# Edge sums of a graph layer: rows as three bfloat16 parts, one-hot matrices as the stationary side

## The chip, the core and the metric

The kernel runs on one core of a Trainium2 chip. The metric is the device time of one execution in microseconds (us). The core's engines are PE (TensorE, matrix products), DVE (VectorE), ACT (ScalarE), POOL (GpSimd) and SP (SyncE, which here only issues DMAs). Each engine works through its own queue in order; semaphores tie the queues together. PE reads SBUF and writes PSUM, which has eight banks of 512 f32 per partition.

## What is computed

A layer of a graph network on 12500 nodes with 128 features and 200000 edges, sorted by destination. `h` is the layer norm of `x` with negative values cut off. Each node takes the mean of `h` over the sources of its incoming edges; four dense layers follow, and `x` is added.

```python
h = jnp.maximum(_layernorm(x, axis=-1), 0.0)
msgs = h[src]                                        # 200000 x 128
agg = segment_sum(msgs, dst, num_segments=n)
deg = segment_sum(ones, dst, num_segments=n)
agg = agg / jnp.maximum(deg, 1.0)[:, None]
y = relu(agg @ Wg + h @ Ws + bg)                     # 128
y = tanh(y @ W1 + b1)                                # 512
y = tanh(y @ W2 + b2)                                # 512
out = x + y @ W3 + b3                                # 128
```

## The kernel before

All is in `windowed`. (A second function, `general`, runs behind it if a flag says that the edges were not spread as assumed; with these inputs it is skipped.) The 200000 edges are cut into 1563 chunks of 128. Since edges are sorted and eight nodes take 128 edges on average, the edges of chunk c end at nodes near 8c; a window of 144 nodes around it (160 for raw chunks, 88 down to 40 for the last 67 chunks) holds them all.

Setup. x is read in pieces of up to 14 tiles of 128 nodes (line 217). `centre`, `factors` and `scale` (lines 161 to 176) make h out of it with whole-piece DVE operations and a Square and a Sqrt on ACT, and h goes as f32 rows of 512 B to a table in DRAM, `htab` (line 228). `indices` turns the lists of sources and destinations so that a chunk's indices stand in one column (`scol`, `dloc`), with PE transposes of a cast copy (lines 180 to 195).

Gathers. POOL fetches the 128 rows of one chunk with one indirect DMA (`gather`, line 290). No gather from the table may start before the table is written, so POOL is first given 80 chunks whose rows come from x itself ("raw" rows, line 132): ten groups of 8 chunks, every 40 chunks from chunk 256 on. Their layer norm is taken later, in the main loop, by the same `centre`, with the square on DVE (line 168). Behind the raw ones POOL gathers the other 1483 chunks in order, up to 40 chunks ahead of their use.

Aggregation. For a group of 8 chunks DVE builds one-hot matrices in f32 (`onehot`, line 327: edge by window position) and, chunk by chunk, adds the same comparison into a count per block of nodes (line 343). `lane`, the row of positions that is compared, lies in PSUM. PE (`add`) takes the gathered rows as the stationary side and the one-hot as the moving side, so sums come out as features by nodes, in PSUM, in the block's bank or, for chunks that lie across a border, in an edge bank. An f32 product is two instructions in the profile. `count` multiplies the counts by ones, so that every partition has the degrees, and takes the reciprocal; `merged` puts the bank and the edges together and multiplies by it.

Layers. Blocks are 23 of 512 nodes, then 256, 128, 128, 112 and 100. `part0` to `part4` are the dense layers; the pieces of their work are generators that the main loop advances between chunks. From chunk 1312 (QUICK) on a model of time, with `there` for the landing of a gather, decides what goes before the next chunk. The node's own h comes from htab (`own`, `hb`), is turned by PE (`own_turned`); x comes once more for the final addition (`own_part`). PE, ACT's own helpers and SP's DMAs are kept in program order; the other orders are the scheduler's. The flag comes from the sum of all degrees (`total`).

Of the kernel before, what the change touches and what calls it, by code (L numbers as in the profile page):

```python
# [31 lines left out]
P = 128  # L32
# [3 lines left out]
PIECE = 14  # L36
GRP = 8
NRAW = 10
# [4 lines left out]
LEAD = 16  # L43
QUICK = 1312

WINDOWS = ((0, 144), (1496, 88), (1536, 56), (1552, 40))
W_RAW = 160
W_MAX = max(W_RAW, *(w for _, w in WINDOWS))

# [6 lines left out]
def windowed(ctx, tc, x, src, dst, Wg, Ws, bg, W1, b1, W2, b2, W3, b3, out, flag):  # L56
# [12 lines left out]
    LAST = E - (NCH - 1) * P  # L69
    NCOL = NROW * CPR  # L70
    RAW1 = RAW0 + NRAW * STEP
    per = N * P // E
    assert D == P and H % P == 0 and per * E == N * P and RAW0 % GRP == STEP % GRP == 0
    assert all(c % GRP == 0 for c, _ in WINDOWS) and RAW1 <= WINDOWS[1][0]


    def raw(c):
        return RAW0 <= c < RAW1 and (c - RAW0) % STEP < GRP

    def first(w, span=per):
        return (span - w) // 2

    def window(c):
        if raw(c):
            return per * (c - c % GRP) + first(W_RAW, per * GRP), W_RAW
        w = [w for c0, w in WINDOWS if c0 <= c][-1]
        return per * c + first(w), w  # L90
# [12 lines left out]
    rows_in = ctx.enter_context(tc.tile_pool(name="rows_in", bufs=AHEAD))  # L103
    ps_c = ctx.enter_context(tc.tile_pool(name="ps_c", bufs=1, space=PSUM))
    ps_a = ctx.enter_context(tc.tile_pool(name="ps_a", bufs=2, space=PSUM))
    ps_m = ctx.enter_context(tc.tile_pool(name="ps_m", bufs=3, space=PSUM))
    ps_b = ctx.enter_context(tc.tile_pool(name="ps_b", bufs=1, space=PSUM))
# [11 lines left out]
    jp = const.tile([P, P], I32, name="jp")  # L119
    nc.gpsimd.iota(jp, pattern=[[1, P]], base=0, channel_multiplier=-1)  # L120
    lane_i = const.tile([P, W_MAX], I32, name="lane_i")
    nc.gpsimd.iota(lane_i, pattern=[[1, W_MAX]], base=0, channel_multiplier=0)
    row_i = const.tile([P, NROW], I32, name="row_i")
    nc.gpsimd.iota(row_i, pattern=[[per * CPR, NROW]], base=0, channel_multiplier=0)
    q_i = const.tile([P, CPR], I32, name="q_i")
    nc.gpsimd.iota(q_i, pattern=[[per, CPR]], base=first(WINDOWS[0][1]), channel_multiplier=0)

    raw_rows = []
    for g in range(NRAW):
        t = raws.tile([P, GRP, D], F32, name=f"raw{g}")  # L130
        for j in range(GRP):
            nc.gpsimd.indirect_dma_start(  # L132
                out=t[:, j, :], out_offset=None, in_=x,
                in_offset=bass.IndirectOffsetOnAxis(ap=rsrc[:, g, j : j + 1], axis=0),
            )
        raw_rows.append(t)

    ident = const.tile([P, P], F32, name="ident")
    nc.vector.tensor_scalar(ident, jp, 0.0, None, op0=ALU.is_equal)
    ones = const.tile([P, P], BF16, name="ones")  # L140
    nc.vector.memset(ones, 1.0)
    eps = const.tile([P, 1], F32, name="eps")
    nc.vector.memset(eps, EPS)

    shared = ps_c.tile([P, BLK], F32, name="shared")
    lane, row_f = shared[:, :W_MAX], shared[:, W_MAX : W_MAX + NROW]
    stats_raw = shared[:, BLK - 2 * NRAW * GRP :].rearrange("p (s c) -> p s c", s=2)
    assert W_MAX + NROW + 2 * NRAW * GRP <= BLK
# [5 lines left out]
    dloc = const.tile([P, NCOL], F32, name="dloc")  # L154

    def spread(f, k):
        return f[:, :, None].to_broadcast([P, k, D])

    def centre(pool, xt, k, stats, bufs=2):
        nc.vector.tensor_reduce(stats[:, 0], xt, AX.X, ALU.add)  # L162
        nc.vector.scalar_tensor_tensor(xt, spread(stats[:, 0], k), -1.0 / D, xt, op0=ALU.mult, op1=ALU.add)  # L163
        sq = pool.tile([P, k, D], F32, name=f"sq{k}", bufs=bufs)
        if bufs > 1:
            nc.scalar.activation(sq, xt, AF.Square)
        else:
            nc.vector.tensor_tensor(sq, xt, xt, op=ALU.mult)
        nc.vector.tensor_reduce(stats[:, 1], sq, AX.X, ALU.add)  # L169

    def factors(stats):
        nc.scalar.activation(stats[:, 1], stats[:, 1], AF.Sqrt, bias=eps, scale=1.0 / D)
        nc.vector.reciprocal(stats[:, 1], stats[:, 1])

    def scale(h, xt, k, stats):
        nc.vector.scalar_tensor_tensor(h, xt, 0.0, spread(stats[:, 1], k), op0=ALU.max, op1=ALU.mult)  # L176

    with tc.tile_pool(name="setup", bufs=1) as sp, tc.tile_pool(name="ln", bufs=2) as ln:

        def indices(name, a, pad, keep):  # L180
# [10 lines left out]
            for q0 in range(0, CPR, 4):  # L191
                p = ps_m.tile([P, 4, P], F32, name="pm")
                for q in range(4):
                    nc.tensor.transpose(p[:, q, :NROW], rf[:, (q0 + q) * P : (q0 + q + 1) * P], ident[:NROW, :NROW])  # L194
                keep(q0, p[:, :, :NROW].rearrange("p q r -> p r q"))


        def by_row(t):
            return t.rearrange("p (r q) -> p r q", q=CPR)

        def keep_src(q0, p):
            nc.vector.tensor_copy(by_row(scol)[:, :, q0 : q0 + 4], p)

        def keep_dst(q0, p):
            nc.vector.tensor_tensor(
                by_row(dloc)[:, :, q0 : q0 + 4], p, by_row(low)[:, :, q0 : q0 + 4], op=ALU.subtract
            )


        pieces = [(0, 4), (4, PIECE - 4)] + [(t, min(PIECE, NT - t)) for t in range(PIECE, NT, PIECE)]  # L210
        for i, (t0, k) in enumerate(pieces):
# [8 lines left out]
            if i == 1:  # L220
                indices("src", src, 0, keep_src)
            stats = ps_a.tile([P, BLK], F32, name="agg")[:, : 2 * k].rearrange("p (s t) -> p s t", s=2)
            xt = xt[:, :k]
# [4 lines left out]
            nc.sync.dma_start(htab[t0 * P : (t0 + k) * P, :].rearrange("(t p) d -> p t d", p=P), h[:, :k])  # L228

        low = sp.tile([P, NCOL], F32, name="low")
        nc.vector.tensor_copy(row_f, row_i)
        nc.vector.tensor_tensor(
            by_row(low), row_f[:, :, None].to_broadcast([P, NROW, CPR]), q_i[:, None, :].to_broadcast([P, NROW, CPR]),
            op=ALU.add,
        )
        for c0, w in WINDOWS[1:]:
            v = low[:, c0:]
            nc.vector.tensor_scalar(v, v, float(first(w) - window(c0 - 1)[0] + per * (c0 - 1)), None, op0=ALU.add)  # L240
        indices("dst", dst, 2 * N, keep_dst)
        steps, at = (t[:, RAW0:RAW1].rearrange("p (u k) -> p u k", k=STEP) for t in (dloc, low))
        nc.vector.scalar_tensor_tensor(
            steps[:, :, :GRP], rdst, float(first(WINDOWS[0][1]) - first(W_RAW, per * GRP)),
            at[:, :, :1].to_broadcast([P, NRAW, GRP]), op0=ALU.add, op1=ALU.subtract,
        )
# [43 lines left out]
    def gather(c):  # L290
        r = rows_in.tile([P, D], F32, name="rows")
        nc.gpsimd.indirect_dma_start(  # L292
            out=r, out_offset=None, in_=htab,
            in_offset=bass.IndirectOffsetOnAxis(ap=scol[:, c : c + 1], axis=0),
        )
        rows_t[c] = r
# [11 lines left out]
    def raw_stats(i):  # L308
        return stats_raw[:, :, i * GRP : (i + 1) * GRP]

    def raw_scaled(i):
        h = raw_rows[i]
        scale(h, h, GRP, raw_stats(i))
        for j in range(GRP):
            rows_t[RAW0 + i * STEP + j] = h[:, j]


    OHS = 4
    oh_bufs = [const.tile([P, GRP, WINDOWS[0][1]], F32, name=f"oh{i}") for i in range(OHS)]
    counts = {}  # L320

    def onehot(g):
        k = min(GRP, NCH - g * GRP)
        lo, w = window(g * GRP)
        is_raw = raw(g * GRP)
        oh = ed.tile([P, GRP, W_RAW], F32, name="ohr", bufs=2) if is_raw else oh_bufs[g % OHS]
# [5 lines left out]
        for c in range(g * GRP, g * GRP + k):  # L332
            lo, w = window(c)
            for b, (n0, m) in enumerate(blocks):
                a0, a1 = max(lo, n0), min(lo + w, n0 + m)
                if a0 < a1:
                    if b not in counts:
                        counts[b] = ed.tile([P, BLK], BF16, name="deg", bufs=3) if m > P else ed.tile(
                            [P, P], BF16, name="deg_s", bufs=4
                        )  # L340
                        nc.vector.memset(counts[b][:, :m], 0.0)
                    d = counts[b][:, a0 - n0 : a1 - n0]
                    nc.vector.scalar_tensor_tensor(  # L343
                        d, lane[:, a0 - lo : a1 - lo], dloc[:, c : c + 1], d, op0=ALU.is_equal, op1=ALU.add
                    )

    reach = [[] for _ in blocks]
    for c in range(NCH):
        lo, w = window(c)
        for b, (n, m) in enumerate(blocks):  # L350
            if lo < n + m and lo + w > n:
                reach[b].append(c)

# [674 lines left out]
```

## Time and profile before

| | |
|---|---|
| median of 3 runs | 1982.97 us (1982.76 to 1983.64) |
| profiled execution | 1985.8 us |
| its span, first to last instruction | 1983.9 us |
| PE, weight loads, DVE, ACT, POOL busy | 69%, 40%, 55%, 11%, 75% |
| mean granted PE clock | 0.893 |
| bytes read and written in HBM | 125.05 MB, 12.82 MB |
| queue of the gathers | 50016 packets, 102.53 MB, 20.5% of the 16 DMA engines' span |

A group in the profile has its line, engine, operation, output and inputs with their shapes and types, and the number of instructions; behind the bar stand the busy time in us and the mean ns of one, and behind the next the engine's idle time just before them, with what ended most of it. In the timeline a line starts with the start and the duration in us; in brackets stands the idle time before it and its releaser. PEld is the loading of a stationary side, POOL's record of an indirect DMA is its issuing and not the transfer.

### The profile page before, as it was taken

How to read it: one execution, taken by the hardware profiler on the slowest of the kernel's cores; microseconds unless marked ns; L12 is line 12 of the kernel's file. 1: busy time of each engine (PE TensorE's matmuls, PEld its weight loads, DVE VectorE, ACT ScalarE, POOL GpSimd, SP SyncE). 2: the span in 40 equal slices, each digit the busy share in tenths (PEclk: the TensorE clock that was granted, in tenths of full speed). 3: DMA queues.
4: the chain of work that ended last, by engine and by line, in shares of the span. 5: the costliest groups of instructions: out<-in, count | busy, mean ns of one | idle time of the engine just before them, and what ended most of it. 6: DMA issues, size and time to landing. Idle time of an engine off the chain costs nothing.

```text
span 1983.9 us, 16321 instructions
## 1 busy us (share of the span) xinstructions
PE 1374.1 (69%) x4838; PEld 793.6 (40%) x4838; DVE 1100.5 (55%) x2649; ACT 219.0 (11%) x352; POOL 1486.8 (75%) x1571
## 2 busy tenths in 40 slices
PE   0056547777778877777676776767767778888797
PEld 0034333434444444344333343333333434444466
DVE  7974856547766586536365363552644625554441
ACT  1100010011111111101001011010110111011022
POOL 7777777777777777777777777777777777777774
PEclk9999858799989898988989989989889898788697
DMA  8822222222222222222222222222222222222221
GB/s 214 234 52 63 55 52 63 53 69 52 69 69 68 54 69 69 69 53 68 69 53 68 53 69 68 53 69 60 62 68 53 69 76 64 60 74 64 53 61 42
DMA packets 120040, 139.10 MB, mean 70 GB/s; under 512 B 30743, under 2 KB 94099, under 8 KB 119749
## 3 DMA queue, kind: packets, MB, share of 16 engines
q0 software_dynamic: 50016, 102.53, 20.5%
q1 hardware_dynamic: 66766, 32.13, 5.9%
q10 hardware_dynamic: 3160, 3.31, 0.6%
q8 instruction: 40, 0.66, 0.1%
q14 instruction: 58, 0.47, 0.1%
HBM read 125.05 MB, written 12.82 MB: 69 GB/s over the span
## 4 chain that ended last, share of the span: by engine, by line
DMA 31%; issue 30%; PE 24%; POOL 8%; DVE 7%; ACT 1%; SPq 0%; POOLq 0%; DVEq 0%
DMA rows<-htab,scol 29%; PE pm L279 13%; POOL rows L292 8%; PE agg L279 7%; PE edge L279 3%; DVE deg L343 2%; PE pt L282 1%; DVE oh L327 1%; DMA xt<-in_x_dram 1%; DVE agg L162 1%; DVE h L176 1%; DVE agg L169 1%; DVE xt L163 0%; ACT h L303 0%; DVE rd L364 0%
## 5 line engine op out<-in xcount | busy, mean ns | idle before, releaser
L292 POOL DMA_INDIRECT rows<-htab,scol x1483 | 1408.6, 950 | 451.9 <-issue 280.1
L279 PE MATMUL agg<-oh,rows 128*128 128x144 f32 (+3 forms) x2122 | 562.7, 367 | 359.1 <-DMA rows<-htab,scol 327.0
L279 PEld LDWEIGHTS agg<-oh,rows 128*128 128x128 f32 x2122 | 392.2, 226 | 736.6 <-DMA rows<-htab,scol 549.2
L279 PE MATMUL pm<-h,w 128*128 128x512 f32 (+4 forms) x1344 | 653.7, 585 | 15.6 <-ACT h L303 15.6
L343 DVE SCALAR_TENSOR_TENSOR deg<-shared,dloc,deg 128x144 bf16<-128x144 f32 (+17 forms) x1921 | 565.7, 326 | 27.1
L327 DVE TENSOR_TENSOR oh<-shared,dloc 128x1152 f32<-128x1152 f32 (+2 forms) x186 | 245.2, 1318 | 207.4 <-PE agg L279 195.7
L279 PE MATMUL edge<-oh,rows 128*128 128x144 f32 (+2 forms) x844 | 223.7, 355 | 138.4 <-DMA rows<-htab,scol 136.8
L279 PEld LDWEIGHTS edge<-oh,rows 128*128 128x128 f32 x844 | 146.4, 212 | 303.0 <-DMA rows<-htab,scol 233.1
L279 PEld LDWEIGHTS pm<-h,w 128*128 128x128 f32 x1344 | 226.5, 208 | 33.7 <-ACT h L303 17.5
L544 DVE TENSOR_TENSOR o<-pt,xb 128x512 f32<-128x512 f32 x23 | 15.9, 691 | 284.8 <-PE pt L282 284.8
L303 ACT ACTIVATE h<-pm,b2c 128x512 f32<-128x512 f32 (+4 forms) x112 | 70.9, 633 | 704.1 <-PE pm L279 704.1
L362 DVE TENSOR_SCALAR rd<-pm 128x512 f32<-128x512 f32 (+4 forms) x28 | 17.4, 623 | 168.2 <-PE pm L279 168.2
L303 ACT ACTIVATE h<-pm,b1c 128x512 f32<-128x512 f32 (+4 forms) x112 | 70.4, 633 | 242.6 <-PE pm L279 242.1
L132 POOL DMA_INDIRECT raw<-in_x_dram,rsrc x80 | 77.3, 966 | 25.7 <-issue 23.8
L426 DVE TENSOR_TENSOR mT<-agg,sums 128x136 f32<-128x136 f32 (+6 forms) x57 | 15.4, 269 | 138.5 <-PE agg L279 134.7
L364 DVE RECIPROCAL rd<-rd 128x512 f32<-128x512 f32 (+4 forms) x28 | 81.8, 2920 | 0.0
L194 PE MATMUL pm<-ident,idx_f 98*128 98x98 f32 x32 | 6.0, 374 | 80.1 <-DVE idx_f L190 79.7
L306 ACT COPY hT<-pt 128x512 f32<-128x512 f32 (+1 forms) x25 | 14.4, 578 | 306.0 <-PE pt L282 293.6
L194 PEld LDWEIGHTS pm<-ident,idx_f 98*128 98x128 f32 x32 | 5.1, 224 | 80.7 <-issue 49.4
L303 ACT ACTIVATE h<-pm,bgc 128x512 f32<-128x512 f32 (+4 forms) x28 | 17.7, 633 | 166.0 <-PE pm L279 166.0
L279 PE MATMUL pm<-hT,ws 128*128 128x512 f32 (+4 forms) x56 | 29.7, 617 | 0.0
L279 PE MATMUL pm<-mT,wg 128*128 128x512 f32 (+4 forms) x56 | 29.1, 605 | 0.3 <-DVE mT L428 0.3
(66 smaller groups left out, 420.3 us busy)
## 6 DMA issues: line engine op xcount, KB each, us to landing
rows<-htab,scol POOLq DMA_INDIRECT x1483, 2.5
hb<-htab SPq DMA_DIRECT2D x24, 256.0 KB, 4.4
xb<-in_x_dram SPq DMA_DIRECT2D x23, 256.0 KB, 5.0
out_dram<-o SPq DMA_DIRECT2D x23, 256.0 KB, 2.7
htab<-h SPq DMA_DIRECT2D x6, 896.0 KB, 5.5
xt<-in_x_dram SPq DMA_DIRECT2D x5, 896.0 KB, 9.3
raw<-in_x_dram,rsrc POOLq DMA_INDIRECT x80, 5.2
w<-in_L_gnn_W_dram ACTq DMA_DIRECT2D x1, 1024.0 KB
```

The lines of the kernel that those rows point to most:

```text
L132: nc.gpsimd.indirect_dma_start(out=t[:, j, :], out_offset=None, in_=x, in_offset=bass.IndirectOffsetOnAxis(ap=rsrc[:, g, j : j + 1], axis=0),)
L162: nc.vector.tensor_reduce(stats[:, 0], xt, AX.X, ALU.add)
L169: nc.vector.tensor_reduce(stats[:, 1], sq, AX.X, ALU.add)
L176: nc.vector.scalar_tensor_tensor(h, xt, 0.0, spread(stats[:, 1], k), op0=ALU.max, op1=ALU.mult)
L279: tc.keep_in_program_order(nc.tensor.matmul(*a, **k))
L282: tc.keep_in_program_order(nc.tensor.transpose(*a, **k))
L292: nc.gpsimd.indirect_dma_start(out=r, out_offset=None, in_=htab, in_offset=bass.IndirectOffsetOnAxis(ap=scol[:, c : c + 1], axis=0),)
L303: tc.keep_in_program_order(nc.scalar.activation(*a, **k))
L327: nc.vector.tensor_tensor(oh[:, :k, :w], lane[:, None, :w].to_broadcast([P, k, w]), dloc[:, g * GRP : g * GRP + k][:, :, None].to_broadcas ...
L343: nc.vector.scalar_tensor_tensor(d, lane[:, a0 - lo : a1 - lo], dloc[:, c : c + 1], d, op0=ALU.is_equal, op1=ALU.add)
L362: nc.vector.tensor_scalar(rd[:, :m], dg[:, :m], 1.0, None, op0=ALU.max)
L364: nc.vector.reciprocal(rd[:, :m], rd[:, :m])
```

## The change

- The table holds each h as three bfloat16 parts whose sum is h, so a row is 3 x 128 bfloat16, 768 B. Layer norm statistics come from `bn_stats` and `bn_aggr`, tile by tile; ACT's ReLU with a scale and a shift per node makes h in PSUM, four tiles to a bank; ACT copies give the parts, DVE subtractions the rest. Pieces are 16 tiles.
- Raw groups are 11 in place of 10 (88 chunks); their norm goes by the same `moments` and a ReLU on ACT.
- Chunks come in groups of 13 (8 for raw ones; the last three groups have 6, 4 and 3). DVE builds one-hots in bfloat16 of 120 nodes from the group's first node (a per-group number, `firsts`, from a product with a matrix whose first row is ones). PE takes the one-hot as the stationary side and the gathered rows, with a column of ones behind them, as the moving side: sums come out as nodes by features, with the in-degree in the last column.
- When a group is complete DVE clips the degree at 256 (`in_deg`) and adds the three parts (`sums`); `put`, three chunks later (one, in the last 16), multiplies both by a 0/1 matrix (`place`, and its bfloat16 copy by ACT, `place_b`) that moves them to their nodes, features by nodes again, with the degree on every partition. DVE adds that to the block's `placed`, in SBUF. `merged` takes the maximum with 1, the reciprocal (into PSUM) and the product.
- A block is started when all groups that reach it have been put. The count per chunk, the edge banks and `count` are gone.
- The node's own h is made from x by ACT (`own_turned`); x is read once for that and for the final addition. Gathered rows lie in 6 fixed buffers of 8.

The core of the diff:

```diff
-PIECE = 14
+PIECE = 16
-NRAW = 10
+NRAW = 11
-LEAD = 16
+LEAD = 6
+KMAX = 13
+MARGINS = ((0, 68), (1496, 40), (1536, 24), (1552, 16))
+LAST = (6, 4, 3)
...
-    htab = dram.tile([NP, D], F32, name="htab")
+    htab = dram.tile([NP, SPLIT], BF16, name="htab")
...
+    def moments(pool, xt, k, mv):
+        st = pool.tile([P, PIECE, 6], F32, name="st")
+        for t in range(k):
+            nc.vector.bn_stats(st[:, t, :], xt[:, t, :D])
+            nc.vector.bn_aggr(mv[:, t, :], st[:, t, :])
+
+    def factors(mv, scale, off):
+        nc.scalar.activation(scale, mv[:, :, 1], AF.Sqrt, bias=eps)
+        nc.vector.reciprocal(scale, scale)
+        nc.vector.scalar_tensor_tensor(off, mv[:, :, 0], -1.0, scale, op0=ALU.mult, op1=ALU.mult)
...
-            centre(ln, xt, k, stats)
-            factors(stats)
-            h = ln.tile([P, PIECE, D], F32, name="h")
-            scale(h[:, :k], xt, k, stats)
+            moments(ln, xt, k, mv)
+            factors(mv[:, :k], rstd[:, t0 : t0 + k], shift[:, t0 : t0 + k])
+            h3 = ln.tile([P, PIECE, 3, D], BF16, name="h3")
+            for a in range(0, k, QUAD):
+                n = min(QUAD, k - a)
+                h = bank()
+                for t in range(n):
+                    at = t0 + a + t
+                    nc.scalar.activation(
+                        h[:, t, :], xt[:, a + t, :], AF.Relu, bias=shift[:, at : at + 1], scale=rstd[:, at : at + 1]
+                    )
+                for j in range(2):
+                    nc.scalar.copy(h3[:, a : a + n, j, :], h[:, :n, :])
+                    left = h3[:, a : a + n, 2, :] if j else h[:, :n, :]
+                    nc.vector.tensor_tensor(left, h[:, :n, :], h3[:, a : a + n, j, :], op=ALU.subtract)
...
     def onehot(g):
...
+        nc.vector.tensor_scalar(near[:, :k], dsts, first, None, op0=ALU.subtract)
...
         nc.vector.tensor_tensor(
             oh[:, :k, :w], lane[:, None, :w].to_broadcast([P, k, w]),
-            dloc[:, g * GRP : g * GRP + k][:, :, None].to_broadcast([P, k, w]), op=ALU.is_equal,
+            near[:, :k][:, :, None].to_broadcast([P, k, w]), op=ALU.is_equal,
         )
...
+        nc.vector.tensor_scalar(
+            place[:w, : hi - lo], shift_lane[:w, : hi - lo], float(lo), first[:w], op0=ALU.add, op1=ALU.is_equal
+        )
+        place_b = ed.tile([P, PLACE], BF16, name="place_b", bufs=4)
+        act.copy(place_b[:w, : hi - lo], place[:w, : hi - lo])
...
+    def add(c):
...
+        pe.matmul(acc[g][:w, :n], ohs[g][:, c - c0, :w], rows, start=(c == c0), stop=(c == c0 + k - 1))
+        if c < c0 + k - 1:
+            return
...
+        nc.vector.tensor_scalar(in_deg[:w], sums[:w, n - 1 : n], 256.0, None, op0=ALU.min)
+        if u is None:
+            nc.vector.tensor_reduce(
+                total_of[:w], sums[:w, :SPLIT].rearrange("p (s d) -> p d s", s=3), AX.X, ALU.add
+            )
...
+    def put(g):
...
+        pe.matmul(scr[:, 1, : hi - lo], in_deg[:w].to_broadcast([w, P]), place_b[:w, : hi - lo], start=True, stop=True)
+        pe.matmul(scr[:, 0, : hi - lo], total_of[:w], place[:w, : hi - lo], start=True, stop=True)
...
+                to = placed[b][:, :, a0 - n0 : a1 - n0]
+                nc.vector.tensor_tensor(to, scr[:, :, a0 - lo : a1 - lo], to, op=ALU.add)
...
     def merged(b, mT):
...
+        nc.vector.tensor_reduce(total[:, b : b + 1], both[:1, 1, :m], AX.X, ALU.add)
+        nc.vector.tensor_scalar(both[:, 1, :m], both[:, 1, :m], 1.0, None, op0=ALU.max)
+        nc.vector.reciprocal(rd[:, :m], both[:, 1, :m])
+        nc.vector.tensor_tensor(mT[:, :m], both[:, 0, :m], rd[:, :m], op=ALU.mult)
...
-            now = max(now, there) + 0.27
+            now = max(now, there) + 0.3
+        while waiting and waiting[0][0] <= c:
+            put_at[waiting[0][1]] = c
+            put(waiting.pop(0)[1])
+            now += 0.8
         add(c)
+        if c in ends:
+            waiting.append((c + (3 if c < NCH - 16 else 1), ends[c]))
+        if c == NCH - 1:
+            while waiting:
+                put(waiting.pop(0)[1])
```

More of the change, by code (lines that the diff above doesn't have):

```diff
@@ L171, in factors @@
[L171 to L176, printed above, removed]
+    nc.vector.tensor_copy(shift_lane, jp)
+    NROWS = AHEAD // GRP + 1
+    rows_bufs = [const.tile([P, GRP, SPLIT + 2], BF16, name=f"rows{i}") for i in range(NROWS)]
+    for t in rows_bufs:
+        nc.vector.memset(t[:, :, SPLIT:], 1.0)
@@ L233, in windowed @@
[L233 to L242, printed above, removed]
@@ L594, in windowed @@
     own(1)
-    own(2)
     own_turned(0)
```

390 lines of the change are left out of this document (186 added, 204 removed).

## The prediction, made before the change was run

> **What bounds the kernel now.** I read the chain that ended last first, but it is a poor guide here: it names DMA (31%) and "issue" (30%), because each gather's landing is followed by the next one's. The costliest groups say more, and then the timeline of the GpSimd engine (POOL), which issues one gather for each chunk of 128 edges.
>
> ```profile
> L292 POOL DMA_INDIRECT rows<-htab,scol x1483 | 1408.6, 950 | 451.9 <-issue 280.1
> L132 POOL DMA_INDIRECT raw<-in_x_dram,rsrc x80 | 77.3, 966 | 25.7 <-issue 23.8
> L279 PE MATMUL agg<-oh,rows 128*128 128x144 f32 (+3 forms) x2122 | 562.7, 367 | 359.1 <-DMA rows<-htab,scol 327.0
> L343 DVE SCALAR_TENSOR_TENSOR deg<-shared,dloc,deg 128x144 bf16<-128x144 f32 (+17 forms) x1921 | 565.7, 326 | 27.1
> ```
>
> POOL: 1408.6 + 451.9 + 77.3 + 25.7 = 1963.5 us, 99% of the span of 1983.9 us. The idle part is no waiting: it is 0.30 us before every gather, whoever is named as its releaser. The POOL timeline:
>
> ```profile
> 102.34 0.95 POOL L132 DMA_INDIRECT raw<-in_x_dram,rsrc  x1 [0.30 <-issue]
> 103.59 0.94 POOL L132 DMA_INDIRECT raw<-in_x_dram,rsrc  x1 [0.30 <-issue]
> 104.84 0.94 POOL L292 DMA_INDIRECT rows<-htab,scol  x1 [0.30 <-DVE deg L343]
> ...
> 1964.13 0.94 POOL L292 DMA_INDIRECT rows<-htab,scol  x1 [0.30 <-issue]
> ```
>
> One gather each 1.25 us, without a hole, from 3.20 us to 1965.07 us. In all 1563 gathers, only 25 records are over 0.97 us; above 0.945 us each they hold 9.2 us together. So the span is three parts: 3.2 us before the first gather; 1563 x 1.2495 + 9.2 = 1962; and 18.8 us behind the last. PE (69%), VectorE (DVE, 55%) and ScalarE (ACT, 11%) lie under the gathers.
>
> What are the 25? The timeline of all engines around the longest, and around one in the setup:
>
> ```profile
> 29.33 1.22 DVE L190 CAST idx_f<-idx_raw 98x2048 f32<-98x2048 int32 x1
> ...
> 29.58 1.78 POOL L132 DMA_INDIRECT raw<-in_x_dram,rsrc  x1 [0.30 <-issue]
> ...
> 210.94 2.07 POOL L292 DMA_INDIRECT rows<-htab,scol  x1 [0.30 <-issue]
> 210.98 1.20 DVE L168 TENSOR_TENSOR sq<-raw 128x1024 f32<-128x1024 f32 x1
> ```
>
> A gather that starts under one of three DVE forms ends about 0.95 us after that operation, not after its own start: the cast (two hits, 1.55 us in all), the square of raw rows by itself, L168 (8 hits, 5.7 us), and products with both inputs in SBUF, L428 (14 hits, 1.7 us); 0.15 us is the first gather. One-hot builds, degree updates, reductions and the 3.33 us reciprocals are never caught so.
>
> The two ends. DMA queue of SyncE (SP) in the setup: the last table row is written by 89.5 us, when the first read of htab goes out, 15 us before POOL needs it (104.84). And behind the last gather:
>
> ```profile
> 73.54 11.54 SPq L228 DMA_DIRECT2D htab<-h  x2
> 89.52 4.84 SPq L288 DMA_DIRECT2D hb<-htab  x4
> ...
> 1970.50 0.47 PE L279 MATMUL pm<-mT,wg 128*128 128x100 f32 x2 [0.30 <-DVE mT L428]
> ...
> 1971.40 5.85 PE L279 MATMUL pm<-h,w 128*128 128x100 f32 x48 [0.43 <-ACT h L303]
> ...
> 1978.04 0.29 DVE L547 TENSOR_TENSOR o<-pt,xs 100x128 f32<-100x128 f32 x1 [7.59 <-PE pt L282]
> ```
>
> Earlier aggregations begin 2.55 us after their gather's start (chunk 1555: gathered at 1955.39, used at 1957.94). So the last lands at L = 1966.7. The last block's wg product starts at L+3.8.
>
> **The change part by part.** The profiled run's span is 1983.9 us (1985.8 with what lies around it); the median of the runs is 1982.97, 0.9 under the span. I sum against the span and take off 0.9.
>
> Number of gathers: 88 + 1475 = 1563, as before. Zero.
>
> Price of a gather: a row becomes 768 B. No gather here has another size than 512 B, so the bounds are wide: zero if POOL's time goes by rows; +50% of 0.945 us, 1475 x 0.47 = +697 us, if it goes by bytes. Below zero I exclude, since no work is taken from it. I take zero: raw and table gathers, into rows spaced 4 KB and 512 B apart in a partition, both take 0.945 us, and the queue's packets (50016 / 1563 = 32 for a gather, 2 KB each) look like four rows for each half of the 16 engines' work. The 16 DMA engines are 20.5% busy with gathers; 1.5 times that is 31%, no bound.
>
> The Trainium skill (DMA: Bandwidth & Descriptors, SWDGE vs HWDGE vs iDMA) has one descriptor pair for each DMA operation and packets of preferably up to 4096 B; four rows of 768 B are 3072 B. By that the price stays; no run here shows it yet.
>
> DVE holding POOL up: the squares go (5.7 us), since bn_stats has one input, and so do the products with two SBUF inputs (1.7): the new ones read the reciprocal from PSUM. The casts stay (1.55). New is a maximum on 512 f32 in SBUF, once per block, about 0.40 us by the cast's rate (1.22 us for 2048, 0.13 us of it fixed), 23 times. If it acts as the cast, a third of them (0.40 / 1.25) meet a gather's start and cost half their length: 23 x 0.32 x 0.2 = 1.5 us; if as the reciprocals, nothing. The near subtractions (120 of 13 elements, some 0.1 us) add up to 0.5. With 1.55 + 1.5 + 0.5 and the first gather's 0.15: 3.7 of 9.2, so -5.5 us (-7.5 to 0).
>
> The Trainium skill (SBUF — State Buffer, section SBUF: two separate sides) makes f32 copies between SBUF tensors lock GpSimd out, and operations with two SBUF inputs against one that reads SBUF. The trace agrees for casts and squares; by the rule alone the maximum would count, with the 1.5 us taken.
>
> Setup: POOL is free for the table after 3.2 + 88 x 1.25 + one cast's 0.8 = 114 us. The table is written later than before. Per piece of 16 tiles, DVE: a reduction is 0.165 us + 1.035 ns per element (0.69 for 512, 2.02 for 1792), and independent ones start 0.08 earlier than the last ends; so bn_stats 0.21 + bn_aggr 0.09 = 0.30, x16 = 4.8; eight subtracts of 512 at 0.61 (0.69 - 0.08) = 4.9; factors 0.4: 10.1 us. ACT: ReLU of 128 by the Square and Sqrt rows 0.34, x16 = 5.4 (most wait for the one before in the same bank); eight copies at 0.59 = 4.7; Sqrt 0.25: 10.4 us. They feed each other: ReLU, copy, subtract, copy, subtract. The bounds for a piece are 10.4 (all overlapped) and 20.5 (none). Also x for a piece waits for its buffer and then 9.3 us (median now) to land. Nothing like it is in the trace; I take 13, nearer the lower end, since four banks allow groups in flight and statistics stand between the subtracts in the built order. The first 16 tiles: x there at 17.9, statistics and the index work (memset 1.8, cast 1.2) to 26, then some 16 us of chain: 42 (14 tiles are sent at 35.5 now). Five pieces more: 42 + 65 = 107. The write of 1.5 MB takes longer than 5.5 us (now 0.9 MB), between 6.3 by rows and 9.4 by bytes: 8. The last two tiles come within it. Table complete at 115.5, POOL waits 1.5 us and, with its restart, 2 (bounds: 42 + 52 + 8 = 102, no wait; 42 + 102 + 9 = 153, wait 39).
>
> Main loop: per chunk PE does one bf16 pass over 386 columns in place of two f32 instructions (0.37 each); DVE loses the 566 us of degree updates and gains per 13 chunks a one-hot of 1560 elements (1.35 us for 1152 now: 1.8), a placement of 256 (0.4), a reduction of 384 (0.56), the add of 512 (0.69): 3.5 us in 16.2. ACT gains a copy of 256 (0.37) per group and four ReLUs per block. All stay under the gathers; gathers run up to 40 chunks, 50 us, ahead, which hides PE's waits for put. SP loses 25 loads of htab, and the x loads come earlier: a load is used a block later than sent. Zero; without that cover each stall of PE would count, a put's about 1.5 us.
>
> Tail, from L, in PE's built order. Block 26 needs the group that ends at chunk 1555, so its wg product comes behind chunk 1559, L-3.6 (before: 1957.24, L-9.5). Chunk 1562 is added at L+0.35 to L+0.6, behind five of block 26's products. Then in_deg and the reduction (0.14 + 0.56, two hops): L+1.4; the two placing matmuls: L+1.9. Now PE's order has 14 of block 26's second-layer products, ws, and three of the third layer before block 27's wg: 18 x 0.27 (100 columns take 2 x 0.122 from the x48 row, 112 a tenth more) = 4.9, and 0.4 waiting for a PSUM buffer that holds the reciprocal until mT: L+7.2. DVE's own part (add 0.2, sum 0.24, maximum 0.2, reciprocal 0.75, product 0.27, and hops, 1.9 us: mT at L+3.9) hides under it. From there the same 7.8 us to the last output and its store. So 7.2 - 3.8 = +3.4 (bounds: +0.5, if only DVE's chain counts, wg at L+4.3, and +5).
>
> Sum: 0 - 5.5 + 2 + 3.4 = -0.1. Span 1983.8, time 1982.9: no change.
>
> **The rivals.**
> - Faster: the setup is ready before 114 us (a piece takes under 12.7), and the new maximum holds nothing: -7 + 0 + 2 = -5, 1978. For: 15 us of slack now, and 10 us added by eight more raw gathers; against: PE's order in the tail is fixed.
> - Slower, the setup becomes the bound: ACT and DVE wait for each other and for x, a piece takes 16 us. Then 42 + 80 + 8 = 130, POOL waits 16, and -5.5 + 16 + 3.4 = +13.9: 1997. It decides from a piece time of 13.5, where the sum passes +4. For: DMA engines are 84 to 105% busy until 75 us, with 3.2 MB to be added. Against: POOL can hide all up to 114.
> - Slower, larger rows cost POOL: 2% of 0.945 us is already +28 us (2010), the whole byte ratio 2680.
>
> **How the numbers follow.** A difference under 0.2%, 4 us, counts as no change. Chances: no change 0.35 (1979 to 1987), faster 0.28, late setup 0.26, dearer gathers 0.08, other losses 0.03 (a stall in the loop). So faster 0.28, same 0.35, slower 0.37. The range leaves out the dearer gathers, a quarter of the late setups and a little below: 1976 to 2000.
>
> **What would show it.** POOL's gathers at 1.25 us for the table rows too; if not, the third rival. A hole before the first table gather near 114 us and its length give the setup's term. Records over 0.97 us: I expect some 10, 4 us in all, none at raw rows. Behind the last landing, wg at L+7.2 with PE busy on block 26's products before it; if PE idles there instead, the tail step is wrong. Holes at 0.30 us elsewhere that grow would show a stall in the loop, and the forecast wrong.

## The result, and the profile after

The changed kernel takes 1988.67 us (median of 15 runs, 1986.35 to 1990.52), the kernel before 1983.02 (15 runs, 1980.97 to 1989.02). The ratio is 1.0026, with a 95% interval of 1.0018 to 1.0034: 5.6 us slower, where no change (under 4 us) was forecast. The time lies inside the stated range of 1976 to 2000 us, whose upper part was meant for a late setup, which did not come. The profiled execution took 1988.29 us, with a span of 1986.5.

The costliest groups of the changed kernel (line, engine, operation, count | busy us, mean ns of one | idle before), and then its queue of gathers (packets, MB, share of the 16 engines):

```profile
L321 POOL DMA_INDIRECT rows<-htab,scol x1475 | 1395.8, 946 | 449.3 <-issue 340.9
L308 PE MATMUL grp<-rows,oh 128*120 128x386 bf16 (+1 forms) x1475 | 540.2, 383 | 555.3 <-DMA rows<-htab,scol 540.4
L146 POOL DMA_INDIRECT raw<-in_x_dram,rsrc x88 | 84.4, 959 | 28.3 <-issue 26.2
```

```profile
q0 software_dynamic: 73616, 150.87, 28.9%
```

POOL is still the spine: 1395.8 + 449.3 + 84.4 + 28.3 = 1957.8 us. A gather of 768 B rows costs it what one of 512 B rows did, with 47 packets (73616 / 1563) in place of 32; a packet has 2.05 KB on average in both. The timeline of POOL and VectorE (start, length, engine, line, what):

```profile
113.10 0.94 POOL L146 DMA_INDIRECT raw<-in_x_dram,rsrc  x1 [0.30 <-issue]
114.35 0.95 POOL L321 DMA_INDIRECT rows<-htab,scol  x1 [0.30 <-issue]
...
778.31 0.40 DVE L427 TENSOR_SCALAR placed<-placed 128x512 f32<-128x512 f32 x1
778.39 1.15 POOL L321 DMA_INDIRECT rows<-htab,scol  x1 [0.30 <-issue]
...
1958.22 0.94 POOL L321 DMA_INDIRECT rows<-htab,scol  x1 [0.30 <-issue]
```

The gather at 778.39 was held up by VectorE's maximum of line 427 and took 1.15 us in place of 0.94. There is no hole where POOL turns to the table, and the last gather starts at 1958.22, 5.9 us earlier than in the profile of before (1964.13). With the same 2.55 us to its first use, the last landing is at L = 1960.8; the last packet of the gathers ended there too, at 1960.83. The span ends 25.7 us after that; before it ended 17.2 us after L = 1966.7. All of the loss is there. The work of each engine between L and the end, before and then after (window, length, busy us of PE, weight loads, VectorE, ScalarE and POOL with counts, granted clock, DMA share, GB/s):

```profile
1966.68:1983.90 17.22, 9.86 (x79) 8.90 (x78) 0.92 (x5) 4.29 (x13) 0.00 (x0) 0.88 0.05 11
```

```profile
1960.77:1986.50 25.73, 17.76 (x119) 15.22 (x118) 4.37 (x16) 6.79 (x21) 0.00 (x0) 0.84 0.04 11
```

PE has 7.9 us more work left when the last rows land, and the stretch is 8.5 us longer. What that work is, PE's timeline shows:

```profile
1956.67 0.35 PE L308 MATMUL grp<-rows,oh 128*64 128x386 bf16 x1
1956.95 1.38 PE L308 MATMUL pm<-h,w 128*128 128x128 f32 x10
...
1961.88 0.37 PE L308 MATMUL pm<-mT,wg 128*128 128x112 f32 x2
...
1965.07 0.34 PE L308 MATMUL grp<-rows,oh 128*40 128x386 bf16 x1
...
1967.82 5.23 PE L308 MATMUL pm<-h,w 128*128 128x112 f32 x30 [0.44 <-ACT h L332]
1972.89 0.38 PE L308 MATMUL pm<-mT,wg 128*128 128x100 f32 x2
```

The wg product opens a block's layers. Block 26 (112 columns) opens at 1961.88, L+1.1; before it opened at L-9.5. So the layers of two blocks follow the landing, not of one. Chunk 1562, landed at L, is added at 1965.07, L+4.3, and block 27's wg comes at L+12.1, where before it came at L+3.8. PE is late even before L: chunk 1555 was gathered at 1949.50 and used at 1956.67, 7.2 us later. Part of this began at the put of the group of two chunks, whose in_deg stood on VectorE behind block 25's reciprocal, while PE waited 1.40 us. The timeline of both engines there:

```profile
1946.16 0.96 DVE L428 RECIPROCAL pm<-placed_s 128x128 f32<-128x128 f32 x1
...
1947.03 0.14 DVE L392 TENSOR_SCALAR in_deg<-grp 32x1 bf16<-32x1 f32 x1
...
1947.22 0.20 PE L308 MATMUL scr<-place_b,in_deg 32*128 32x80 bf16 x1 [1.40 <-DVE in_deg L392]
```

In the profile of before PE was late too, at a granted clock of 0.50 from 1957 to 1966, and added the last chunk at L+2.9:

```profile
1969.62 0.30 PE L279 MATMUL agg<-oh,rows 128*128 128x20 f32 x2
```

### The profile page after: what moved, and what is told of

Same layout as the page of the kernel before. It is cut to its first block, busy times and chain, and to the rows that moved or that the text cites. A ratio compares the mean times of both kernels' runs of the same rounds, so it can differ in the third digit from the quotient of the medians.

```text
span 1986.5 us, 13250 instructions
## 1 busy us (share of the span) xinstructions
PE 1285.7 (65%) x3742; PEld 608.6 (31%) x3742; DVE 694.4 (35%) x1528; ACT 378.0 (19%) x785; POOL 1480.9 (75%) x1569
## 3 DMA queue, kind: packets, MB, share of 16 engines
q0 software_dynamic: 73616, 150.87, 28.9%
## 4 chain that ended last, share of the span: by engine, by line
issue 34%; PE 29%; DMA 21%; POOL 12%; DVE 3%; ACT 2%; POOLq 0%; ACTq 0%; DVEq 0%
DMA rows<-htab,scol 20%; PE pm L308 18%; POOL rows L321 8%; PE grp L308 7%; POOL raw L146 4%; PE scr L308 3%; PE pt L311 1%; DVE pm L428 1%; ACT hb L332 1%; DVE oh L360 1%; ACT h L332 1%; DVE sums L394 0%; DVE mT L429 0%; DVE place L367 0%; ACT place_b L335 0%
## 5 line engine op out<-in xcount | busy, mean ns | idle before, releaser
L321 POOL DMA_INDIRECT rows<-htab,scol x1475 | 1395.8, 946 | 449.3 <-issue 340.9
L308 PE MATMUL grp<-rows,oh 128*120 128x386 bf16 (+1 forms) x1475 | 540.2, 383 | 555.3 <-DMA rows<-htab,scol 540.4
L308 PEld LDWEIGHTS <-oh 128*120 128x120 bf16 (+1 forms) x1475 | 217.3, 151 | 728.4 <-issue 582.2
L360 DVE TENSOR_TENSOR oh<-shared,near 128x1560 bf16<-128x1560 f32 (+3 forms) x122 | 197.3, 1617 | 0.0
L335 ACT CAST place_b<-place 120x256 bf16<-120x256 f32 (+6 forms) x133 | 51.5, 389 | 653.9 <-DVE place L367 583.2
L420 DVE TENSOR_TENSOR placed<-scr,placed 128x512 f32<-128x512 f32 (+24 forms) x186 | 88.0, 500 | 121.7 <-PE scr L308 121.6
L332 ACT ACTIVATE h<-pm,b1c 128x512 f32<-128x512 f32 (+4 forms) x112 | 70.2, 632 | 217.8 <-PE pm L308 217.5
L146 POOL DMA_INDIRECT raw<-in_x_dram,rsrc x88 | 84.4, 959 | 28.3 <-issue 26.2
L308 PE MATMUL scr<-place,sums 120*128 120x256 f32 (+6 forms) x266 | 97.0, 453 | 1.0 <-DVE sums L394 1.0
L428 DVE RECIPROCAL pm<-placed 128x512 f32<-128x512 f32 (+1 forms) x24 | 78.9, 3287 | 10.7 <-ACT h L332 10.1
L394 DVE TENSOR_REDUCE sums<-grp 120x128 f32<-120x384 f32 (+3 forms) x122 | 66.7, 547 | 0.0
L367 DVE TENSOR_SCALAR place<-shared,firsts 120x256 f32<-120x256 f32 (+6 forms) x133 | 60.6, 455 | 0.0
L308 PEld LDWEIGHTS scr<-place,sums 120*128 120x128 f32 (+3 forms) x266 | 51.9, 242 | 26.6 <-issue 15.2
```

The costliest lines, as they stand in the source:

```text
L146: nc.gpsimd.indirect_dma_start(out=t[:, j, :D], out_offset=None, in_=x, in_offset=bass.IndirectOffsetOnAxis(ap=rsrc[:, g, j : j + 1], axis=0),
L308: tc.keep_in_program_order(nc.tensor.matmul(*a, **k))
L321: nc.gpsimd.indirect_dma_start(out=r[:, :SPLIT], out_offset=None, in_=htab, in_offset=bass.IndirectOffsetOnAxis(ap=scol[:, c : c + 1], axi ...
L332: tc.keep_in_program_order(nc.scalar.activation(*a, **k))
L335: tc.keep_in_program_order(nc.scalar.copy(*a))
L360: nc.vector.tensor_tensor(oh[:, :k, :w], lane[:, None, :w].to_broadcast([P, k, w]), near[:, :k][:, :, None].to_broadcast([P, k, w]), op=AL ...
```

## The experiments

There were 18 runs. In fifteen of them PE used a chunk's rows 42 to 57 us after their gather's start (medians; 2.6 us in the profile of before), with the unchanged kernel too, so POOL waited for free buffers: in e1, the kernel before as it is, it had 266 gaps over 0.4 us, 377 us together, where otherwise it has one, and the kernel before took 2304.5 to 2328.5 us (medians). The rows were not late: a table gather's last packet ended 2.2 us (median) after the gather's start in e1 as in the profile of before. The waits were long, even those within one engine, as e3 shows further down; why they were is not shown. Such times say nothing on an end that POOL sets; what those records show all the same is said where it is used. These are called runs with long waits here. L is always the start of the last gather + 2.55 us.

**Groups that end where blocks end (e3c).** The changed kernel; the last 54 chunks are cut so that a group ends at the last chunk that reaches a block: eight groups in place of seven. Blocks 24, 25 and 26 can start 10, 7 and 4 chunks earlier.

```diff
-LAST = (6, 4, 3)
+LAST = (8, 8, 7, 7, 13, 4, 4, 3)
```

> The aligned cut of the last 54 chunks, a third time, on a chip where gathers are issued each 1.25 us throughout. Theory (late start of the last blocks): chunk 1562 is added at L+0.5 to L+1, wg of the last block at L+5, the time falls by 7 to 8 us against the changed kernel, to 1981, 2 us under before. Rival 1 (too much work on PE at the end, one more put with it): 1988 to 1990. Rival 2 (puts wait behind reciprocals in VectorE's queue): 1986 to 1987, with idle PE named after in_deg or mT.

1984.35 us (11 runs) against 1981.89 for the kernel before on this chip: 1.0009 (1.0000 to 1.0018). That is 2.5 us above the kernel before, where the changed kernel lay 5.6 above it, so 3.2 us are won back. The profile (span 1980.9): work behind L, and PE.

```profile
1960.83:1980.90 20.07, 11.61 (x71) 9.89 (x70) 2.96 (x11) 3.93 (x12) 0.00 (x0) 0.84 0.04 11
```

```profile
1951.88 0.47 PE L308 MATMUL pm<-mT,wg 128*128 128x112 f32 x2
...
1962.31 0.34 PE L308 MATMUL grp<-rows,oh 128*40 128x386 bf16 x1
...
1965.80 0.47 PE L308 MATMUL pm<-mT,wg 128*128 128x100 f32 x2 [0.58 <-DVE mT L429]
1966.76 7.46 PE L308 MATMUL pm<-h,w 128*128 128x100 f32 x48 [0.49 <-ACT h L332]
```

Block 26 opens at L-8.9, the last chunk is added at L+1.5 (the theory had L+0.5 to L+1), and the last wg comes at L+5.0, as the theory said, now waiting for mT. The time fell with one put more, so rival 1 falls; what that put costs by itself is not shown. Rival 2 is not excluded as a part: with the other cut no put stands behind a reciprocal for long, and the 1.40 us shown above are gone too. PE's work behind L is down by 6.2 us and the stretch by 5.7. The median gained less than the 7 to 8 us expected, and less than this profile: its own execution, 1982.74 us, lies 1.6 under the median. Part of the rest stands in the last line: the last block's 48 instructions take 7.46 us at a granted clock of 0.77, where the profile of before had 5.85 at 1.00.

Some 5 us of loss behind the landing are left: the time is 2.5 us above the kernel before, although the last gather starts some 2.4 us earlier (1958.28; 1960.81 and 1960.56 in e4d and f1d, which have before's gathers). A lower clock is a rival for this part: over the whole span it was 0.824 to 0.836 in these runs and 0.824 to 0.835 in the changed kernel's, but 0.891 to 0.902 in those of the kernel before on this chip. No run changes the clock alone, so its share stays open.

Two earlier runs of this kernel had long waits and say nothing on its tail: 2383.16 us against 2310.73 (e3) and 2404.2 against 2328.48 (e3b). Where these 72 and 76 us went is read further down.

> The changed kernel with the last 54 chunks cut so that a group ends where a block's last node is reached (groups of 8, 8, 7, 7, 13, 4, 4, 3 in place of 13, 13, 13, 2, 6, 4, 3): one group more, and the last three blocks but one can start 10, 7 and 4 chunks earlier. Theory (the last blocks start late because whole groups have to end first, and their products then stand on PE in front of the last chunk): chunk 1562 is added at L+0.5 to L+1, wg of the last block at L+5, the time falls by 7 to 8 us, to 1981. Rival 1 (PE has too much work at the end, the putting of sums included): one more put, no gain, 1988 to 1990. Rival 2 (VectorE's queue: puts wait behind reciprocals): gain of 2 us at most, with idle PE named after in_deg or mT.

> The aligned cut of the last 54 chunks again, where gathers are issued each 1.25 us. Theory (late start of the last blocks): chunk 1562 is added at L+0.5 to L+1, wg of the last block at L+5, the time falls by 7 to 8 us against the changed kernel, to 1981, 2 us under before. Rival 1 (too much work on PE at the end, one more put with it): 1988 to 1990. Rival 2 (puts wait behind reciprocals in VectorE's queue): 1986 to 1987, with idle PE named after in_deg or mT.

**A late start put into the kernel before (e4d).** No groups and no puts; three blocks merely start later, by the chunks that whole groups cost.

```diff
-        lead = LEAD if c < QUICK else 2
+        lead = (LEAD if c < QUICK else 2) + {24: 11, 25: 8, 26: 3}.get(done, 0)
```

> The kernel before with three of its last blocks started 11, 8 and 3 chunks later, by itself. Theory (the late start is the loss): wg of the last block at L+9 to L+12, 5 to 8 us more than before. Rival (the changed kernel's puts or a lower clock are the loss): within 2 us of before. If gathers are again not issued each 1.25 us, the time says nothing about the tail.

1981.52 us (12 runs) against 1982.15: 0.9997 (0.9989 to 1.0006). The theory falls in this form. The window behind L says why:

```profile
1963.36:1979.90 16.54, 10.07 (x83) 9.29 (x82) 1.01 (x5) 4.53 (x14) 0.00 (x0) 0.92 0.05 12
```

Block 26's wg still came at 1957.44, L-5.9: without puts its sums are there when the chunk count allows the start. PE even waited 1.04 us for a landing at 1961.88. The delay was absorbed, and no more work than before lay behind L. So the number of chunks is not the measure; where the block really opens is.

Three earlier runs had long waits: 2308.65 us against 2310.73 (e4), 2323.02 against 2328.48 (e4b) and 2323.87 against 2325.73 (e4c). They decide nothing.

> The kernel before, with nothing added but a later start of three of its last blocks: 11, 8 and 3 chunks, as the groups of 13 make it. Theory (the late start is the loss): wg of the last block moves from L+3.8 to L+9 to L+12, and the time rises by 5 to 8 us, to 1988 to 1991. Rival (the loss is the changed kernel's own: the puts, their wait for VectorE, a lower clock): within 2 us of before, 1983 to 1985.

> The kernel before with three of its last blocks started 11, 8 and 3 chunks later, again where gathers are issued each 1.25 us. Theory (the late start is the loss): wg of the last block at L+9 to L+12, 5 to 8 us more than before, 1988 to 1991. Rival (the changed kernel's puts or a lower clock are the loss): 1983 to 1985.

> The kernel before with three of its last blocks started 11, 8 and 3 chunks later, on a chip where gathers are issued each 1.25 us throughout. Theory (the late start is the loss): wg of the last block at L+9 to L+12, 5 to 8 us more than before, 1987 to 1990. Rival (the changed kernel's puts or a lower clock are the loss): within 2 us of before.

**The true lateness put into the kernel before (f1d).** The same edit with 12, 11 and 8 chunks, chosen so that the three blocks open where the changed kernel really opens them.

```diff
+        lead = (LEAD if c < QUICK else 2) + {24: 12, 25: 11, 26: 8}.get(done, 0)
```

> The kernel before with its last three blocks but one started 12, 11 and 8 chunks later, so that their wg products come near L-28, L-12 and L as in the changed kernel; once more, where gathers are issued each 1.25 us. Theory (what counts is the layer products of two blocks left behind L, whatever made them late): wg of the last block at L+9 to L+12, 5 to 8 us more than before. Rival (the puts and their chain through VectorE are the loss by themselves): wg at L+3 to L+5, within 2 us of before.

1989.02 us (10 runs) against 1982.72: 1.0028 (1.0019 to 1.0038), 6.3 us more without one put, and at the clock of the kernel before (0.889 to 0.900 over the span in these runs, 0.889 to 0.904 in before's). Behind the landing the changed kernel lost some 8.1 us, its 5.6 and the 2.5 that its gathers gained, so a late start alone is enough for some three quarters of that. The window behind L, and PE:

```profile
1963.11:1988.60 25.49, 17.97 (x107) 16.44 (x106) 1.02 (x5) 6.72 (x20) 0.00 (x0) 0.71 0.04 10
```

```profile
1964.51 0.65 PE L279 MATMUL pm<-mT,wg 128*128 128x112 f32 x2
...
1969.45 0.61 PE L279 MATMUL pm<-mT,wg 128*128 128x100 f32 x2
1969.86 6.06 PE L279 MATMUL pm<-h,w 128*128 128x112 f32 x36
```

Blocks 24, 25 and 26 open at L-28.1, L-12.0 and L+1.4 (the changed kernel: L-27.9, L-12.0, L+1.1). PE has 18.0 us of work behind L, as after (17.8; busy time, which a lower clock stretches), and the stretch is 25.5 us (25.7). The marker was wrong: the last wg came at L+6.3, not L+9 to L+12, because this schedule lets it pass most of block 26's products, which then stand behind it. So the sum of work behind L fits the time, and the place of one product does not. In this profile the clock granted behind L was 0.71, so the stretch owes some of its length to that; this execution, 1990.62 us, is the slowest of the ten, 1.6 over their median.

Three earlier runs had long waits: 2300.7 us against 2309.17 (f1), 2307.31 against 2308.14 (f1b) and 2309.12 against 2304.59 (f1c). With long waits the start of a block cost nothing that shows.

> The kernel before with its last three blocks but one started where the changed kernel really starts them, counted from the landing of the last gather: 12, 11 and 8 chunks later than now, so that their wg products come near L-28, L-12 and L. (With 11, 8 and 3 chunks they came at L-30, L-16 and L-6, and the time stayed.) Theory (what counts is the layer products of two blocks left behind L, whatever made them late): wg of the last block at L+9 to L+12, 5 to 8 us more than before. Rival (the puts and their chain through VectorE are the loss by themselves): wg at L+3 to L+5, within 2 us of before.

> The kernel before with its last three blocks but one started 12, 11 and 8 chunks later, so that their wg products come near L-28, L-12 and L as in the changed kernel; a second time, where gathers are issued each 1.25 us. Theory (what counts is the layer products of two blocks left behind L, whatever made them late): wg of the last block at L+9 to L+12, 5 to 8 us more than before. Rival (the puts and their chain through VectorE are the loss by themselves): wg at L+3 to L+5, within 2 us of before.

> The kernel before with its last three blocks but one started 12, 11 and 8 chunks later, so that their wg products come near L-28, L-12 and L as in the changed kernel; a third time, where gathers are issued each 1.25 us. Theory (what counts is the layer products of two blocks left behind L, whatever made them late): wg of the last block at L+9 to L+12, 5 to 8 us more than before. Rival (the puts and their chain through VectorE are the loss by themselves): wg at L+3 to L+5, within 2 us of before.

**One boundary alone (f2).** `LAST = (4, 4, 4, 3)`: as many groups as the changed kernel, only block 26 starts earlier.

> The changed kernel with one group boundary moved: the last groups are 13, 4, 4, 4, 3 chunks in place of 13, 2, 6, 4, 3, as many as now, so that block 26 can start after chunk 1552 in place of 1556; the blocks before it start as late as in the changed kernel. Theory (the products of block 26 stand on PE between the last sums and the last block): its wg product comes at L-3 to L-5 in place of L+1.1, the last block's at L+7 to L+8, and the time falls by 4 to 5 us against the changed kernel. Rival 1 (the backlog that blocks 24 and 25 leave, and VectorE's queue, decide): the last wg at L+10 to L+12, 0 to 2 us. Rival 2 (the puts' own chain): L+12, no gain.

It fell among the runs with long waits (2415.97 us against 2322.82). Which of the three blocks weighs most was not settled.

**The square of raw rows on ScalarE (e2).** The kernel before with one instruction moved.

```diff
-            nc.vector.tensor_tensor(sq, xt, xt, op=ALU.mult)
+            nc.scalar.activation(sq, xt, AF.Square)
```

> The kernel before, with one instruction moved: the square of the raw rows, 8 times 1.2 us on VectorE, is computed by ScalarE. Theory (a gather that starts under that square ends 0.95 us after it): no record over 0.97 us is left at raw rows, and the time falls by 5.7 us times the share of hits, 5 to 6: 1977 to 1978. Rival (the long records are the gathers' own, or any engine's write to SBUF holds them up): 1983, with the long records still there, beside ScalarE's squares.

All four runs (e2, e2b, e2c, e2d) had long waits, so the time where POOL sets the end was not measured, and whether this version beats both kernels stays open. There the edit costs 0.3 to 0.4% (1.0041, 1.0033, 1.0036 and 1.0029), for a cause that stays open. But POOL's own records can be read all the same: without a hold-up a table gather takes 943.2 ns in e1 and 944.8 in the profile of before. The groups of POOL, without the edit (e1) and with it (e2), on the same chip:

```profile
L292 POOL DMA_INDIRECT rows<-htab,scol x1483 | 1406.2, 948 | 746.6 <-issue 309.2 <-remote 175.4 <-PE agg L279 135.3
```

```profile
L292 POOL DMA_INDIRECT rows<-htab,scol x1483 | 1399.3, 944 | 757.4 <-issue 319.2 <-remote 188.3 <-PE agg L279 145.9
```

6.9 us less. Without the edit 19 records are over 0.97 us (9.2 us above 0.945 together), eight of them at raw rows (6.5 us); with it there are 8 (2.5 us), none at raw rows. The other three profiles with the edit have 5 to 9 long records (1.6 to 2.5 us). That the square held these gathers up is shown; that 5 to 6 us of time would follow is not.

The three repeats:

> The kernel before with the raw rows' square on ScalarE, again where gathers are issued each 1.25 us. Theory (the gathers held up by that square cost what their records show): 8 records of 1.7 to 2.1 us are gone, the time falls by 5 to 6 us, to 1977 to 1978. Rival (what POOL loses there it gets back later, or does not set the end): 1982 to 1983.

> The kernel before with the raw rows' square on ScalarE, where gathers are issued each 1.25 us throughout. Theory (the gathers held up by that square cost what their records show): the 8 long records are gone, the last gather starts 5 to 6 us earlier, and the time falls by as much, to 1976 to 1977. Rival (the end is set by something else, PE's backlog for one): no change.

> The kernel before with the raw rows' square on ScalarE, alone, where gathers are issued each 1.25 us. Theory (the gathers held up by that square cost what their records show, 5.1 to 5.7 us in three profiles of kernels that have it): the 8 long records are gone, the last gather starts at 1955 to 1957, and the time falls by 5 to 6 us to 1976 to 1978, under both kernels. Rival (the end is set by something else, PE's backlog for one): no change.

**The kernel before once more (e1).**

> The kernel before, unchanged, profiled once more: its span was 1983.9 us, its median time 1983.0 (a span of some 1981.2). If the profiled execution lay high by chance, the new span is 1980 to 1982, with fewer or shorter gathers over 0.97 us than the 9.2 us counted, or a shorter tail behind the last landing than 17.2 us. If the span is again 1983 to 1985, the profile of before is typical and the changed kernel's loss is only 2.6 us.

> The kernel before, profiled once more where gathers are issued each 1.25 us throughout. Its first profile had a span 2 to 3 us over the median run's, and PE at a granted clock of 0.50 from 1960 to 1965 us, with the last chunk added at L+2.9. If that low clock was chance, the span is now 1980 to 1982, the last chunk is added within L+1.5 and wg comes at L+2 to L+3. If the last gather itself starts earlier than 1963, the long records vary from run to run instead.

Both runs had long waits (2310.65 and 2318.71 us), but e4d and f1d have before's gathers unchanged, without them: their last gathers start at 1960.81 and 1960.56, with 17 and 21 long records (7.8 and 7.7 us). The first profile, at 1964.13, was 3 us later than these.

**What long waits do to the changed kernel (e3, e3b, f2).** These three, the changed kernel with other last groups, took 1.034, 1.031 and 1.042 times the kernel before. POOL's timeline of e3, where the raw gathers end:

```profile
112.51 0.94 POOL L146 DMA_INDIRECT raw<-in_x_dram,rsrc  x1 [0.31 <-issue]
183.36 0.94 POOL L321 DMA_INDIRECT rows<-htab,scol  x1 [69.91 <-DMA b1c<-in_L_gnn_b_dram]
```

The releaser named is only the last event by the profile. What POOL needed was the table: SP's queue issued the last table writes up to 177.8, and the first load behind them at 182.66. 70 us of waiting, of 72 us lost (2383.16 against 2310.73); 71.6 and 70.2 us in the other two. The kernel before, on the same chip, waited 0.73 us at this place. VectorE's timeline in e3's setup, where the mean and variance of a tile (`bn_aggr`) follow its `bn_stats`:

```profile
46.15 0.26 DVE L186 BATCH_NORM_STATS2 st<-xt 128x6 f32<-128x128 f32 x1
48.85 0.18 DVE L187 BATCH_NORM_AGGREGATE mv<-st 128x2 f32<-128x6 f32 x1 [2.44 <-remote]
```

The second takes the result of the first on the same engine; in the changed kernel's own profile no such pair has a gap. In e3's setup VectorE stood idle for 51 us in front of `bn_aggr`, which the kernel before does not have. A late setup that makes POOL wait is the prediction's second rival, but in a size that it did not have, and in large part by VectorE's waits for itself.

## Why the prediction was wrong, step by step

- *Number of gathers:* right, 1563.
- *Price of a gather:* taken as zero, and right. Without long records a table gather takes 945.5 ns after, and 943.5 to 944.8 ns in the profiles of before, e4d and f1d; but 512 B rows took 943.2 ns in e1 and 945.4 in e1c, so this difference is no more than executions of the same kernel show. The packets did not stay at four rows each: 47 for a gather, where 32 were taken for granted. The Trainium skill (DMA: Bandwidth & Descriptors, SWDGE vs HWDGE vs iDMA) led to that with its packets of up to 4096 B; the price it left unchanged did stay.
- *DVE holding POOL up:* right in kind. 9 long records, 2.5 us (some 10 and 4 us, with a sum of 3.7, were forecast): the first gather, two casts, and 6 of the 23 maxima, 1.2 us (1.5 taken); none at raw rows. So the rule of the Trainium skill (SBUF — State Buffer, SBUF: two separate sides), by which the prediction let the maximum count, holds here. The size was off against the median: the gain of 5.9 us stands against a profile whose gathers ended 3 us late. Against e4d and f1d the last gather comes 2.5 us earlier.
- *Setup:* +2 was mis-sized; it is 0. The table was complete by 105.05, when the first load queued behind its writes went out, not at 115.5; a piece took some 11 us, not 13.
- *Main loop:* zero, right; every gap before a gather is 0.30 us.
- *Tail:* this step failed. It said "Chunk 1562 is added at L+0.35 to L+0.6" and wg "L+7.2", +3.4 in all with +5 as the upper bound. Measured: L+4.3, L+12.1 and +8.5. The step took PE's order from the build but started its count at the landing, as if PE were level with the gathers there. PE was not level even in the profile of before, where the last chunk was added at L+2.9. For the changed kernel a sum over the stretch shows it: from block 25's wg (1948.7) to L are 12.1 us, and to be level PE needs in them 25 products of that block at 0.26 us (6.6, by the x10 line: 1.31 us to the next instruction), 12 row matmuls at 0.28 (3.4) and two puts at 0.42 (0.8): 10.8 us where the clock is full, 13.7 at the 0.79 granted from 1950 to 1960. No product of block 26 fits in. The late opening of 26 was in the text ("Block 26 needs the group that ends at chunk 1555"), its products behind L too, but not the backlog that block 25, itself 13.7 us later relative to L, leaves in front of them. That a late start costs most of it is shown by f1d (6.3 of some 8.1 us) and e3c (3.2 won back); what the rest is, the lower clock or the chain of the puts, stays open.
- *The sum:* by the profile pair -5.9 + 8.5 = +2.6, as the spans say (1986.5 - 1983.9); against typical gathers -2.5 + 8.5 = +6.0, near the 5.6 of the medians. That the size of the saving fits the profile pair is luck, as the item on VectorE says.

The forecast of no change rested on a gain of 5.5 and losses of 5.4. The gain was half as large against the median run, one loss did not come, and the other was two and a half times its size.

## What to carry to other kernels

When a change makes results ready in coarser lots, look at the last lots: let each end where a consumer's needs end, and count what work is left behind the last transfer. A delay costs nothing while the engine has idle time before that transfer to make it up (block 26 opened 3.6 us later relative to L in e4d, for 0 us), and it costs where that time is used up (10.9 us later in f1d, for 6.3 us); so add up that engine's work between the late start and the last landing before pricing the order behind it. And before subtracting a saving from one profile, compare that execution's time with the median: here more than half of the saving was that profile's own bad luck.

## What the runs showed of the hardware

- POOL's time for an indirect gather of 128 rows, without hold-up, was 945.5 ns for rows of 768 B and 943.2 to 945.4 ns for rows of 512 B (before, e1, e1c, e4d, f1d), while the packets of a gather rose from 32 to 47 and the busy share of the DMA engines from 20.5 to 28.9%.
- The unchanged kernel took 1980 to 1989 us in some runs and 2292 to 2338 us in others. In the second kind the packets of a gather ended as early (2.2 us after its start) and POOL's gathers took as long (943.2 ns in e1), but PE used the rows some 42 us after their gather. The changed kernel was 0.3% slower in the first kind, its variants 3 to 4% in the second.
- In the second kind a `bn_aggr` stood up to 5.8 us behind the `bn_stats` before it on the same engine (e3); in the changed kernel's own profile it never waited.
- The clock granted to PE over the span was 0.824 to 0.835 in the 15 executions of the changed kernel and 0.889 to 0.904 in those of the kernel before on the chips of e3c, e4d and f1d; why is not shown.
- The gathers held up by VectorE vary by execution: 9.2, 7.8 and 7.7 us in three profiles of the same loop.
